# Layer 3's mask in the largest-score pass as a matmul with a plain maximum, and reciprocals of the weights' sums with queries in partitions

## The chip, the core and the metric

The kernel runs on one core of a Trainium2 chip. The metric is the device time of one execution in microseconds; for the kernel before there are three executions and one profiled one. TensorE is the matrix engine, VectorE, ScalarE and GpSimd work on 128 partitions each, and SyncE (SP) issues most DMAs. In the profile's rows they are PE (PEld for its weight loads), DVE, ACT, POOL and SP.

## What is computed

Four layers run over x of shape (8, 256, 128), with a context of shape (8, 512, 128). Each is a gated cross-attention and a gated feed-forward part, both on a layer-normalised x:

```python
x = x + tanh(g_xattn[l]) * attention_l(layernorm(x), ctx, ctx, ...)
x = x + tanh(g_ffn[l]) * feed_forward_l(layernorm(x), ...)
```

Layers 2 and 3 are what the change touches. Both have 16 heads of 8 features, 256 queries and 512 keys to a batch. Layer 2 has a mask of integers, a bias by position, and a softmax whose denominator has 1 added; layer 3 has two boolean masks:

```python
# layer 2
scores = where(mask == 0, -inf, q @ k.T / sqrt(8) + bias)
e = exp(scores - max(scores))
attn = e / (1.0 + sum(e))
# layer 3
energy = where(padding_mask & tri_mask, q @ k.T * 128**-0.5, finfo.min)
attn = softmax(energy)
```

Layer 2's feed-forward part is a mixture of 15 experts and a shared one, here all computed for all rows and weighed (16 passes for each group of 512 rows). Layer 3's is a linear layer with ternary weights and one common scale for its rounded input.

## The kernel before

Layer 0 and the setup run first, up to about 350 us. From then on `pipeline` (line 916) writes out one interleaved order of layers 1 to 3 in Python. The unit of work is (layer, batch, g), where g is one half of the heads: 48 units. Three streams go through the units: `prepare` (projections and loads of operands), four steps later `largest` (the row maxima of the scores), and four steps after that `attend` (scores again, now with keys in partitions, exponentials and the product with the values). A unit takes four steps of the loop at line 936, and in each step `largest` and `attend` come twice, each time with one score tile of 128x1024. Work that isn't of these streams is put in between: `later(1, f)` (line 979) puts a function on the list `due`, and `run_due` runs the list in the order in which it was filled, one step later, after the first `attend` tile of that step and ahead of its `largest` tile; `front` holds the preparation of the next batch, `back` the feed-forward parts (`int8`, `experts2`, `ternary`), one piece of each twice a step. VectorE, ScalarE, GpSimd and TensorE keep the order in which the instructions are written (`InOrder`, line 36, and `mm`, line 861).

PSUM has three score tiles (`sc`, 128x1024), one bank for small products (`pj`) and one for the product with the values (`av`). A score tile comes free when ScalarE's exponential or VectorE's maximum has read it; attend and largest tiles take turns.

`mask(layer, b)` (line 1397) makes the mask of a batch twice: `bq` with queries in partitions, two blocks of 512 keys, holding 0 or -2**100, and `bk`, its transpose, in bfloat16, with a second copy whose partition halves are swapped (two DMAs). `largest23` (line 1439) makes a score tile of 128 queries x 512 keys for two heads with two matmuls and then, for each head, calls `tensor_tensor_reduce` on VectorE: it adds `bq` to the scores and takes the maximum (each is followed by an instruction that reads the accumulator into `mx`). `largest_rows` (line 1168) turns `mx` by a transpose, splits it in two parts and writes them by DMA as rows of `qx`, so that the attend scores come with the maximum subtracted. `attend23` (line 1466) begins each of its score tiles with four 64x64 matmuls that add `bk` through blocks of an identity, then four score matmuls, and ScalarE's exponential.

`values_of_four` (line 1501) multiplies the exponentials by the values, 32 instructions in the trace for each call, twice a unit; the values are laid out with columns of ones beside them, so the sums of the weights stand in rows of the same result `oS`. After a batch's second unit `normalise` (line 1522) spreads these sums over the features' rows by the 0/1 matrix `sel` (result `pd`, features in partitions, 256 queries along the row), ScalarE copies them to `rec` (adding 1 in layer 2). One step later `scaled` takes the reciprocal of `rec` (128x256) on VectorE and GpSimd multiplies `oS` by it. One step after that `output23` projects. A float32 matmul stands as two instructions in the trace.

Of the kernel before, what the change touches and what calls it, by code (L numbers as in the profile page):

```python
# [10 lines left out]
BF16 = mybir.dt.bfloat16  # L11
# [8 lines left out]
P = 128  # L20
# [11 lines left out]
def bcast(ap, shape):  # L32
    return ap.to_broadcast(list(shape))
# [15 lines left out]
class Flamingo:  # L49
# [866 lines left out]
    def pipeline(self):  # L916
        nc, tc = self.nc, self.tc
        with ExitStack() as st:
            PS = bass.MemoryType.PSUM
            self.p_sc = st.enter_context(tc.tile_pool(name="p_sc", bufs=3, space=PS))  # L920
            self.p_pj = st.enter_context(tc.tile_pool(name="p_pj", bufs=1, space=PS))
            self.p_av = st.enter_context(tc.tile_pool(name="p_av", bufs=1, space=PS))
            self.po = st.enter_context(tc.tile_pool(name="pipe", bufs=2))
            units = [(layer, b, g) for layer in (1, 2, 3) for b in range(NB) for g in range(2)]
            self.due, self.soon, self.back, self.front, self.step, self.kept = [], [], [], [], 0, {}
            streams = {
                n: self.chain(f, units, wait)
                for n, f, wait in (("pr", self.prepare, 0), ("la", self.largest, 4), ("at", self.attend, 8))
            }
            self.fill_tile = lambda: self.t(self.po, "et", [P, 2, 2, S], bufs=5).rearrange(  # L930
                "p a b s -> p (a b s)"
            )[:, 0:SK]
            self.fill2(4)
            for _ in self.ahead(1, 0):
                pass
            for self.step in range(4 * len(units) + 12):

                next(streams["at"])
                self.run_due()
                next(streams["la"])  # L940
                self.run_soon()
                self.some(self.front)
                self.some(self.back)
                next(streams["at"])
                next(streams["pr"])
                next(streams["la"])
                self.fill2(1)
                self.some(self.front)
                self.some(self.back)
            while self.due or self.back:  # L950
                self.step += 1
                self.run_due()
                self.run_soon()
                self.some(self.back)
            self.ternary_end()
# [441 lines left out]
    def mask(self, layer, b):  # L1397


        nc, a = self.nc, self.a  # L1400
        bq = self.t(self.po, "bq", [P, 2, SK], BF16)
        bk = self.t(self.po, "m4", [P, 4, S], bufs=3).bitcast(BF16).rearrange("p (r k) n -> p r (k n)", r=2)

        def load(c):
            if layer == 2:
                tl = self.t(self.po, "mi", [P, SK], I32, bufs=1)
                nc.sync.dma_start(tl, a["mask"][b, c * P : (c + 1) * P, :])
                return tl
            if c == 0:
                tl = self.t(self.po, "pad", [P, SK], U8)  # L1410
                nc.sync.dma_start(tl, a["keep_bk"][b].partition_broadcast(P))
                return tl
            return got

        got = load(0)
        yield
        for c in range(2):
            if layer == 2:
                nc.vector.tensor_scalar(bq[:, c, :], got, 0.0, -BIG, ALU.is_equal, ALU.mult)
            else:  # L1420
                nc.vector.tensor_tensor(bq[:, c, :], self.triq[:, c, :], got, ALU.mult)
                nc.vector.tensor_scalar(bq[:, c, :], bq[:, c, :], 1.0, BIG, ALU.subtract, ALU.mult)
            if c == 0:
                got = load(1)
            yield
        pt = self.pj16()
        for k in range(4):
            for c in range(2):
                self.tp(
                    pt[:, k * S + c * P : k * S + (c + 1) * P], bq[:, c, k * P : (k + 1) * P], self.identb  # L1430
                )
        nc.scalar.copy(bk[:, 0, :], pt)
        for z in range(2):
            h, other = slice(64 * z, 64 * z + 64), slice(64 - 64 * z, 128 - 64 * z)
            nc.sync.dma_start(bk[h, 1, :], bk[other, 0, :])
        self.kept["mask", layer, b] = bq, bk
        yield

    def largest23(self, n, layer, b, g):
        nc = self.nc  # L1440
        qx, kx, _ = self.kept[n]
        bq, _ = self.kept["mask", layer, b]
        rows = 36 if layer == 2 else 32
        mx = self.t(self.po, "mx", [P, 2, 2, 2, 2])
        for j in range(4):
            for c in range(2):
                ps = self.sc()
                for z in range(2):
                    self.mm(
                        ps[:, z, :],  # L1450
                        self.packed(qx, z, 0, rows)[:, j, c * P : (c + 1) * P].bitcast(F32R),
                        self.packed(kx, z, 0, rows)[:, j, :].bitcast(F32R),
                    )
                for z in range(2):
                    junk = self.t(self.po, "junk", [P, SK], BF16, bufs=1)
                    nc.vector.tensor_tensor_reduce(
                        junk, ps[:, z, :], bq[:, c, :], 1.0, -3.0e38, ALU.add, ALU.max,
                        mx[:, c, j // 2, z, j % 2 : j % 2 + 1],
                    )
                if c and j % 2:  # L1460
                    self.later(1, self.largest_rows(
                        mx, j // 2, -1.0, lambda z, k: self.packed(qx, z, rows + k, 1)
                    ))
                yield

    def attend23(self, n, layer, b, g):
# [10 lines left out]
        for j in range(4):  # L1477
            for k2 in range(2):
                ps = self.sc()

                for z in range(2):
                    for o in range(2):
                        h = slice(64 * z, 64 * z + 64)
                        self.mm(
                            ps[64 * o : 64 * o + 64, z, :], self.identb[h, h],
                            bk[h, int(o != z), k2 * SK : (k2 + 1) * SK], True, False,
                        )
                for c in range(2):
                    for z in range(2):
                        at = (2 * k2 + c) * P  # L1490
                        self.mm(
                            ps[:, z, c * S : (c + 1) * S],
                            self.packed(kx, z, 0, rows)[:, j, at : at + P].bitcast(F32R),
                            self.packed(qx, z, 0, rows)[:, j, :].bitcast(F32R), False, c == 1,
                        )
                held[j, k2] = self.weights(ps, scale)
                if k2 and j % 2:
                    self.later(1, self.values_of_four(layer, b, g, j // 2, held, va, oS, oN))
                yield
# [21 lines left out]

    def normalise(self, layer, b, oS, oN):

        nc = self.nc
        pd = self.pj()
        for z in range(2):
            h = slice(64 * z, 64 * z + 64)
            for g in range(2):
                self.mm(pd[h, 0:S], self.sel[:, g, h], oS[:, g, :], g == 0, g == 1)
        rec = self.t(self.po, "rec", [P, S], bufs=1)  # L1530
        nc.scalar.activation(
            rec, pd[:, 0:S], AF.Identity, bias=self.ones[:, 0:1] if layer == 2 else 0.0
        )

        def scaled():
            nc.vector.reciprocal(rec, rec)
            nc.gpsimd.tensor_tensor(oN, oS, bcast(rec.unsqueeze(1), [P, 2, S]), ALU.mult)
            self.later(1, lambda: self.output23(layer, b, oN))

        self.later(1, scaled)  # L1540
# [23 lines left out]
    def experts2(self, tb):  # L1564
# [36 lines left out]
        def hidden(e):  # L1601
            ps = self.sc()
            self.mm2(ps[:, 0, :], self.f2_w[:, 0, e, :], xT)
            return ps
# [15 lines left out]
        def weighed(e, py):  # L1620
# [6 lines left out]
            for t in range(2, 4):  # L1627
# [2 lines left out]
                    self.x[:, t0 + t, :], ALU.mult, ALU.add,  # L1630
                )

        ps = hidden(0)
        pt = self.pj()
        for t in range(4):
            self.tp(pt[0 : E + 1, t * P : (t + 1) * P], comb[:, t, :], self.ident)
        hT = positive(0, ps)
        cT = self.t(po, "cT2", [E + 1, 512], bufs=1)
        nc.scalar.copy(cT, pt[0 : E + 1, :])
        yield  # L1640
        pb = self.sc()[:, 0, :]
# [10 lines left out]
        for e in range(E + 1):  # L1652
            ps = hidden(e + 1) if e < E else self.sc()
            output(e, hT, ps[:, 1, :])
            if e < E:
                hT = positive(e + 1, ps)
            weighed(e, ps[:, 1, :])
            yield


# [180 lines left out]
```

## Time and profile before

| What | Value |
|---|---|
| time, median of 3 runs | 1808.77 us (1801.66 to 1819.17) |
| time of the profiled execution | 1804.63 us |
| its span, first to last instruction | 1802.8 us |
| instructions in the trace | 33356 |
| mean granted TensorE clock | 0.905 |
| layers 1 to 3: first maxima with a mask (layer 2), layer 3's first and last | 922.2, 1358.7, 1757 us |
| attend's exponential, 128x1024 (ScalarE) | 1025 ns |
| reciprocal of 128x256 (VectorE), layers 2 and 3 | 16 of 1747 ns |

The span is that of the profiled execution, and the 1.8 us between it and that execution's time lie outside the instructions. In a group row of the profile come the line of the source (a helper's where it issues), engine, operation, out<-in by tile names, shapes and count; after the bar the busy time of the group, the mean duration of one in ns, and the idle time of the engine ahead of these. Matmuls that run side by side in parts of the array are counted once in the busy time. In a table of stretches each engine has its busy time and, in brackets, its instructions; PEclk is the share of the full clock that the throttle granted. A timeline row has the start, the duration, the engine, and in brackets the idle time ahead of it and what ended it.

### The profile page before, as it was taken

The page shows a single profiled execution, that of the slowest core. Times are in us where ns is not written, and L with a number is a line of the kernel's source. Part 1 is how long each engine was busy: PE and PEld are TensorE (multiplying, and loading weights), DVE is VectorE, ACT ScalarE, POOL GpSimd, SP SyncE. Part 2 cuts the span into 40 slices and gives each one's busy share as a digit, 9 for nine tenths or more (in the row PEclk, how much of TensorE's full clock was granted, in tenths as well). Part 3 has the DMA queues.
Part 4 walks back from the last instruction along what each step waited for, and adds up shares of the span by engine and source line. Part 5 has one row for each costly group of instructions (what it writes and reads, how often), then busy time and mean ns, then how long its engine had stood idle before and what let it go on. Part 6 is the DMA issues. An engine that isn't in the chain of part 4 may idle for free.

```text
span 1802.8 us, 33356 instructions
## 1 busy us (share of the span) xinstructions
PE 1570.0 (87%) x12368; PEld 787.8 (44%) x12368; DVE 1160.3 (64%) x2667; ACT 749.2 (42%) x1244; POOL 741.0 (41%) x1140
## 2 busy tenths in 40 slices
PE   5878578689999999999988889889898999899995
PEld 2333226134544545445554445445444455444442
DVE  7997642245677677676686666575665756666663
ACT  3443332343333232333333545555545555444443
POOL 4896221234656566565562231222232323322211
PEclk9896788899999999999998988989989899888876
DMA  5453232722221122122113331222121211222200
GB/s 190 150 166 113 94 127 76 237 99 100 75 73 54 48 78 77 48 55 94 51 40 104 85 91 44 68 69 54 50 54 37 65 46 44 63 63 63 66 17 25
DMA packets 67974, 142.04 MB, mean 79 GB/s; under 512 B 12882, under 2 KB 28515, under 8 KB 61156
## 3 DMA queue, kind: packets, MB, share of 16 engines
q1 hardware_dynamic: 65842, 136.22, 24.8%
q0 software_dynamic: 1536, 3.15, 1.3%
q8 instruction: 98, 1.61, 0.4%
q10 hardware_dynamic: 434, 0.54, 0.1%
q14 instruction: 64, 0.52, 0.1%
HBM read 83.50 MB, written 51.38 MB: 75 GB/s over the span
## 4 chain that ended last, share of the span: by engine, by line
PE 59%; DVE 20%; issue 6%; ACT 5%; POOL 5%; DMA 3%; SPq 1%; ACTq 0%; DVEq 0%; POOLq 0%
PE sc L863 31%; PE av L863 14%; PE pj L863 8%; DVE junk L46 4%; PE pj L867 3%; DVE ps L46 2%; DVE rec L46 2%; DVE pj L46 2%; DVE x L46 2%; DVE nm L46 1%; PE fl L863 1%; POOL k L46 1%; ACT et L46 1%; DMA kx<-k 1%; ACT total L46 1%
## 5 line engine op out<-in xcount | busy, mean ns | idle before, releaser
L46 ACT ACTIVATE et<-sc 128x1024 f32<-128x1024 f32 (+1 forms) x403 | 404.5, 1005 | 460.8 <-PE sc L863 434.5
L46 DVE CUSTOM_DVE_ANT_0 junk<-sc,bq 128x512 bf16<-128x512 f32 x512 | 350.9, 685 | 43.7 <-PE sc L863 30.0
L863 PE MATMUL av<-et,va 128*32 128x256 f32 (+1 forms) x3072 | 286.1, 439 | 0.8 <-DVE aT L46 0.8
L863 PE MATMUL sc<-qx,kx 64*128 64x256 f32 (+2 forms) x2048 | 275.8, 369 | 3.8 <-DMA qx<-ms 3.8
L863 PE MATMUL sc<-kx,qx 64*128 64x512 f32 (+2 forms) x1024 | 276.5, 576 | 0.4 <-ACT et L46 0.4
L46 POOL TENSOR_TENSOR k<-et 128x512 f32<-128x512 f32 x128 | 162.6, 1271 | 175.4 <-ACT et L46 174.4
L46 DVE TENSOR_REDUCE nm<-sc 128x2 f32<-128x1024 f32 x128 | 156.0, 1219 | 109.8 <-PE sc L863 109.8
L863 PEld LDWEIGHTS sc<-qx,kx 64*128 64x128 f32 (+2 forms) x2048 | 184.0, 197 | 92.5 <-issue 72.3
L863 PEld LDWEIGHTS av<-et,va 128*32 128x32 f32 (+1 forms) x3072 | 139.1, 133 | 113.2 <-issue 55.2
L46 POOL TENSOR_TENSOR x<-row,x 128x256 f32<-128x256 f32 x76 | 55.4, 729 | 274.8 <-ACT row L46 261.5
L46 DVE SCALAR_TENSOR_TENSOR ms<-pj,ms 4x256 fp32r<-4x256 f32 x96 | 39.5, 411 | 186.1 <-ACT ms L46 186.1
L863 PE MATMUL sc<-m,identb 64*64 64x512 bf16 x1024 | 115.0, 438 | 27.0 <-DVE mx L46 21.7
L863 PEld LDWEIGHTS sc<-kx,qx 64*128 64x128 f32 (+2 forms) x1024 | 90.3, 191 | 90.3 <-issue 69.4
L46 DVE RECIPROCAL rec<-av 128x256 f32<-128x256 f32 x64 | 111.8, 1747 | 0.0
L46 POOL TENSOR_TENSOR lnz<-lny 128x2 f32<-128x2 f32 (+1 forms) x129 | 25.0, 194 | 211.0 <-DVE lny L46 198.1
L46 DVE SCALAR_TENSOR_TENSOR x<-sc,comb,x 128x128 f32<-128x128 f32 x128 | 39.0, 346 | 100.1 <-ACT row L46 100.1
L863 PE MATMUL sc<-xT,wb 128*64 128x512 f32 x256 | 69.0, 614 | 24.3 <-DVE x L46 22.4
L46 ACT ACTIVATE total<-sc,f_b 128x512 f32<-128x512 f32 x64 | 44.0, 687 | 106.6 <-PE sc L863 106.6
L46 POOL TENSOR_TENSOR total<-k 128x512 f32<-128x512 f32 x64 | 81.4, 1271 | 5.0
L46 POOL TENSOR_TENSOR aT<-aT,rec 128x512 f32<-128x512 f32 x16 | 20.3, 1271 | 145.0 <-DVE rec L46 145.0
L863 PEld LDWEIGHTS <-identb 64*64 64x64 bf16 x1024 | 34.9, 107 | 95.3 <-issue 89.5
L863 PEld LDWEIGHTS sc<-wb,total 128*64 128x64 f32 x1024 | 61.7, 137 | 33.5 <-issue 33.5
(275 smaller groups left out, 2319.7 us busy)
## 6 DMA issues: line engine op xcount, KB each, us to landing
kx<-k SPq DMA_DIRECT2D x16, 1024.0 KB
va<-v SPq DMA_DIRECT2D x16, 1024.0 KB
k<-fill SPq DMA_DIRECT2D x46, 256.0 KB
v<-fill SPq DMA_DIRECT2D x45, 256.0 KB
pd<-k SPq DMA_DIRECT2D x16, 512.0 KB
kx<-pd SPq DMA_DIRECT2D x64, 128.0 KB
kx<-pd SPq DMA_DIRECT2D x128, 64.0 KB
qx<-pd SPq DMA_DIRECT2D x128, 64.0 KB
```

The lines of the kernel that those rows point to most:

```text
L46: return lambda *args, **kw: self.tc.keep_in_program_order(v(*args, **kw))
L863: self.nc.tensor.matmul(out, lhsT, rhs, start=start, stop=stop)
L867: self.tc.keep_in_program_order(self.nc.tensor.transpose(out, in_, ident))
```

## The change

- **Mask in largest-score tiles of layer 3.** The four mask matmuls of `attend23` become a method `masked`, and `largest23` calls it ahead of its two score matmuls for layer 3, except while the experts run (a flag `in_experts`, set from the first hidden product of `experts2` to its last but one step). In these tiles one `tensor_reduce` with max over 128x2x512 takes the place of the two `tensor_tensor_reduce`. The mask tile `bq` gets a second copy with swapped halves, by two more DMAs, in layer 3.
- **Reciprocals.** `normalise` now makes the sums with queries in partitions: `oS` is the stationary operand and every eighth column of `sel` (16 of them) the moving one. VectorE adds 1 or 0 and takes the reciprocal of 128x32. `scaled` widens each value to 8 columns on ScalarE (128x256), TensorE turns the two blocks against the identity, ScalarE copies the result, and GpSimd multiplies as before. This is for layers 2 and 3.
- **Room.** `pad` shares the tile of layer 2's integer mask, and `cT` that of `xn2`.

```diff
@@ mask
-        bq = self.t(self.po, "bq", [P, 2, SK], BF16)
+        bq = self.t(self.po, "bq", [P, 2, 2 * SK], BF16)
+        bqc = [bq[:, 0, c * SK : (c + 1) * SK] for c in range(2)]
...
-                tl = self.t(self.po, "pad", [P, SK], U8)
+                tl = self.t(self.po, "mi", [P, SK], I32, bufs=1)[:, 0 : SK // 4].bitcast(U8)
...
             h, other = slice(64 * z, 64 * z + 64), slice(64 - 64 * z, 128 - 64 * z)
+            if layer == 3:
+                nc.sync.dma_start(bq[h, 1, :], bq[other, 0, :])
             nc.sync.dma_start(bk[h, 1, :], bk[other, 0, :])
...
+    def masked(self, ps, b2, at):
+        for z in range(2):
+            for o in range(2):
+                h = slice(64 * z, 64 * z + 64)
+                self.mm(
+                    ps[64 * o : 64 * o + 64, z, :], self.identb[h, h], b2[h, int(o != z), at : at + SK],
+                    True, False,
+                )
@@ largest23
                 ps = self.sc()
+                by_pe = layer == 3 and not self.in_experts
+                if by_pe:
+                    self.masked(ps, bq, c * SK)
                 for z in range(2):
                     self.mm(
                         ps[:, z, :],
                         self.packed(qx, z, 0, rows)[:, j, c * P : (c + 1) * P].bitcast(F32R),
-                        self.packed(kx, z, 0, rows)[:, j, :].bitcast(F32R),
+                        self.packed(kx, z, 0, rows)[:, j, :].bitcast(F32R), not by_pe, True,
                     )
-                for z in range(2):
+                if by_pe:
+                    nc.vector.tensor_reduce(mx[:, c, j // 2, :, j % 2], ps, AX.X, ALU.max)
+                for z in () if by_pe else range(2):
@@ normalise
-        for z in range(2):
-            h = slice(64 * z, 64 * z + 64)
+        for c in range(2):
             for g in range(2):
-                self.mm(pd[h, 0:S], self.sel[:, g, h], oS[:, g, :], g == 0, g == 1)
-        rec = self.t(self.po, "rec", [P, S], bufs=1)
-        nc.scalar.activation(
-            rec, pd[:, 0:S], AF.Identity, bias=self.ones[:, 0:1] if layer == 2 else 0.0
+                self.mm(
+                    pd[:, 16 * c : 16 * c + 16], oS[:, g, c * P : (c + 1) * P], self.sel[:, g, 0:P:8],
+                    g == 0, g == 1,
+                )
+        rec = self.t(self.po, "rec16", [P, 2, 16])
+        nc.vector.tensor_scalar(
+            rec.rearrange("p c h -> p (c h)"), pd[:, 0:32], 1.0 if layer == 2 else 0.0, None, ALU.add
         )
+        nc.vector.reciprocal(rec, rec)
 
         def scaled():
-            nc.vector.reciprocal(rec, rec)
-            nc.gpsimd.tensor_tensor(oN, oS, bcast(rec.unsqueeze(1), [P, 2, S]), ALU.mult)
+            wide = self.t(self.po, "recw", [P, 2, P], bufs=1)
+            nc.scalar.copy(
+                wide.rearrange("p c (h f) -> p (c h) f", f=8),
+                bcast(rec.rearrange("p c h -> p (c h)").unsqueeze(2), [P, 32, 8]),
+            )
+            pr = self.pj()
+            for c in range(2):
+                self.mm2(pr[:, c * P : (c + 1) * P], wide[:, c, :], self.ident)
+            rows = self.t(self.po, "rec", [P, S], bufs=1)
+            nc.scalar.copy(rows, pr[:, 0:S])
+            nc.gpsimd.tensor_tensor(oN, oS, bcast(rows.unsqueeze(1), [P, 2, S]), ALU.mult)
             self.later(1, lambda: self.output23(layer, b, oN))
@@ experts2
+        self.in_experts = True
         ps = hidden(0)
...
-        cT = self.t(po, "cT2", [E + 1, 512], bufs=1)
+        cT = self.t(po, "xn2", [P, 4, D], bufs=1).rearrange("p t d -> p (t d)")[0 : E + 1, :]
...
             weighed(e, ps[:, 1, :])
+            self.in_experts = e < E
             yield
```

## The prediction

> **What bounds the kernel now.** I read the page first: busy shares and the chain that ended last.
>
> ```profile
> PE 1570.0 (87%) x12368; PEld 787.8 (44%) x12368; DVE 1160.3 (64%) x2667; ACT 749.2 (42%) x1244; POOL 741.0 (41%) x1140
> ...
> PE 59%; DVE 20%; issue 6%; ACT 5%; POOL 5%; DMA 3%; SPq 1%; ACTq 0%; DVEq 0%; POOLq 0%
> ```
>
> TensorE leads on both counts, but this is an average over stages, so I went to layer 3 alone. The scores of the largest-score pass run there from 1358.7 to 1757 us in 128 tiles, 8 to a unit of (batch, half of the heads). Without experts beside them, units alternate:
>
> ```profile
> core 0: us, PE busy (x) PEld busy (x) DVE busy (x) ACT busy (x) POOL busy (x), PEclk, DMA share, GB/s
> ...
> 1650.70:1670.70 20.00, 18.54 (x203) 10.00 (x202) 15.18 (x43) 11.72 (x19) 1.66 (x3) 1.00 0.25 69
> 1670.70:1695.00 24.30, 22.79 (x155) 9.75 (x154) 15.54 (x46) 10.07 (x14) 11.23 (x33) 0.65 0.23 60
> ```
>
> In both TensorE is busy 93% and VectorE 76% and 64%. The second has fewer matmuls yet takes longer: its granted clock is 0.65. What TensorE waits for between 1562 and 1758 us is little:
>
> ```profile
> engine line waited for: us in total, times, longest us
> PE sc L863 <- DVE mx L46: 9.1, 20, 0.6
> PE pj L867 <- DVE ms L46: 2.1, 4, 0.7
> ```
>
> So VectorE is near the bound only in short stretches of bare score tiles. One such stretch, with the reciprocal beside it, in the timeline:
>
> ```profile
> 1657.44 0.49 PE L863 MATMUL sc<-kx,qx 32*128 32x512 f32 x2
> ...
> 1658.13 0.08 DVE L46 DVE_READ_ACCUMULATOR2_ANT mx<- 128x1 f32 x1
> 1658.27 0.41 PE L863 MATMUL sc<-m,identb 64*64 64x512 bf16 x4 [0.33 <-DVE mx L46]
> ...
> 1658.61 0.50 PE L863 MATMUL sc<-qx,kx 34*128 34x256 f32 x4
> ...
> 1659.04 1.93 PE L863 MATMUL av<-et,va 128*32 128x256 f32 x32
> ...
> 1659.21 1.02 ACT L46 ACTIVATE et<-sc 128x1024 f32<-128x1024 f32 x1 [0.64 <-PE sc L863]
> ...
> 1659.71 1.75 DVE L46 RECIPROCAL rec<-rec 128x256 f32<-128x256 f32 x1
> ```
>
> One 0.33 us wait for the maximum, then the value products (av) follow, and the 1.75 us reciprocal lies wholly beside their 1.93 us and the rows behind them.
>
> **Part 1, the mask of the largest-score pass, on VectorE.** The rows that price it:
>
> ```profile
> L46 DVE CUSTOM_DVE_ANT_0 junk<-sc,bq 128x512 bf16<-128x512 f32 x512 | 350.9, 685 | 43.7 <-PE sc L863 30.0
> L46 DVE TENSOR_REDUCE nm<-sc 128x2 f32<-128x1024 f32 x128 | 156.0, 1219 | 109.8 <-PE sc L863 109.8
> L863 PE MATMUL sc<-m,identb 64*64 64x512 bf16 x1024 | 115.0, 438 | 27.0 <-DVE mx L46 21.7 <-ACT et L46 3.1 <-DVE x L46 2.0
> L46 DVE DVE_READ_ACCUMULATOR2_ANT mx<- 128x1 f32 x512 | 41.5, 81 | 0.0
> L863 PE MATMUL pj<-wr,xT 128*128 128x15 f32 x32 | 4.6, 278 | 0.0
> L863 PE MATMUL pj<-wp,ctxT 128*64 128x128 f32 x256 | 17.5, 279 | 0.0
> ```
>
> Per tile VectorE loses 2 x (685 + 81) = 1532 ns and gains one maximum over 128x1024, which is layer 1's row of 1219 ns: 0.31 us less. How many tiles? The flag leaves out those between an expert's start and its last but one step; counting the experts' matmuls between tiles gives 28 left out, 100 changed: 31 us less VectorE work. As VectorE isn't the bound, that is worth only the waits above: 9.1 us, and about 2 in the earlier changed tiles, **-11 us**.
>
> **Part 1 on TensorE.** Each changed tile gets four 64x64 mask matmuls of the very form of the third row. Taken from start to start, the group of four before the attention scores takes 0.34 us at full clock (1658.27 to 1658.61 above) and 0.57 at half (1587.69 to 1588.26 in the timeline). Of the 100 tiles 78 start at full clock, 22 at half: 78 x 0.34 + 22 x 0.57 = **+39 us**, in TensorE's own order, with nothing to hide behind in units that are 93% busy. Below it can't cost nothing, as the bare stretches leave only the 11 us already taken; above, if all ran at half clock, 57. With the waits gone: **+28 us**.
>
> **Part 2, the reciprocals (layers 2 and 3, 16 batches).** VectorE loses 1.75 us a batch and gains an addition and a reciprocal over 32 columns; no row is that small with 32, but the maximum's followers with 60 columns take 0.22 each, so 0.4 at most. TensorE: before, 8 instructions of 256 columns, 1.09 us busy in the timeline. After, 8 with a 128-column weight and 16 moving columns, nearest to the router's 128x15 (4.6 / 32 = 0.144 each, 1.15 us), and 8 that turn the widened rows (17.5 / 256 = 0.068 each, 0.55 us). That is +0.6 us a batch. ScalarE has two copies of 128x256 (0.37 each) for one of 0.38, with room.
>
> The order matters more. The reciprocal and the multiply were on VectorE and GpSimd, with no TensorE step between. Now `scaled` has ScalarE's widening copy, then TensorE's transposes, which wait for that copy, and TensorE keeps its order. `scaled` was put on the list before the values of the next half of the heads, so it runs ahead of av. ScalarE has, in the same order, the exponential of the tile just scored ahead of the copy. In the timeline av could start at 1659.04; the exponential ends at 1660.23; with 0.37 for the copy and two hand-overs of 0.04 the transposes start at 1660.68. **TensorE stands 1.6 us**, and behind it wait av, then the turning of the maxima, then the next scores. Beside experts the exponential ends 1.1 to 1.5 us after av's start, so 1.6 to 1.9. From below it is nothing if ScalarE had done the exponential by then, which the row excludes; from above 1.9. I take 1.6 for 15 batches: 15 x (1.6 + 0.6) = +33. VectorE catches up in that pause and has no long reciprocal, so I take 0.4 us a batch of later waits for it away, an estimate from the 0.33 wait above: -6. The last batch is alone at the end, where the chain goes through 0.38 + 1.75 us of ScalarE and VectorE: about 0.4 + 0.37 + 0.55 + 0.37 instead, -0.5. Sum **+26 us**.
>
> **Part 3, what costs nothing.** Two more DMAs a batch on SP's queue (the other halves of bq), just ahead of the mask's own copy, which takes 1.17 us for two; the mask is prepared about a unit ahead (20 us) and kx and qx of the next unit queue behind. If that cover fails, about 1.2 us a batch, 9 in all. The shared tile for pad is read 40 us before the next load needs it, and cT in place of xn2 was last read before it.
>
> **The clock.** Windows between changes of the granted clock are 3.4 us long. In a row:
>
> ```profile
> 1581.60:1585.10 3.50, 2.88 (x28) 1.42 (x24) 2.42 (x7) 1.68 (x3) 2.48 (x13) 0.99 0.01 2
> 1585.10:1588.50 3.40, 3.40 (x14) 0.92 (x14) 2.73 (x10) 1.71 (x2) 2.01 (x3) 0.50 0.45 121
> 1588.50:1591.90 3.40, 3.40 (x26) 1.62 (x30) 2.72 (x8) 1.75 (x2) 0.21 (x2) 0.50 0.72 176
> ```
>
> TensorE is busy all through the second and third, and stays at half. It is back at full only after the next window, with 28 of av's matmuls. The Trainium skill, page "TensorE: Matmul & The Clock Gate", Part 1, says that about 3.4 us of sustained work give the full clock and an idle window takes it away. By that rule more matmuls would lift the slow units: of the 110 us at half clock in the changed stretch 42% would be saved (0.34 for 0.57, 0.43 for 0.73, 1.87 for 3.57), 46 us. By the rows, windows that are full of masks and thin scores don't count as work; what returns the clock are full-row matmuls such as av. The measurement decides: I take no gain. The sum by the rule would be 23 + 26 - 46 = +3, by the rows +54.
>
> **Sum.** Span 1802.8 + 28 + 26 = 1856.8, with 1.8 around it (1804.63 less 1802.8) 1858.6. The median of the runs shown is 4 us above the profiled one, so I write **1860**.
>
> **The rivals.**
> 1. *Clock lost as well.* In the full-clock units the window at 1653 has no av; the selection matmuls, 256 columns each, carry it, and the change cuts them to 16. With the pause of 1.6 us it may fall to half until the next av: 6.8 us at half lose 2.9; in some 8 batches 23 us, 1882. For: the window before a fall has next to no av. Against: projections in it stay.
> 2. *The pause is hidden* by waits that would follow anyway: 28 + 15 x 0.6 - 6 = +31, 1836. Against: the slow waits in the table are short.
> 3. *Clock kept, on the other side.* The masks count as work and hold the full clock: +3, 1807, the same. It decides if nearly all 110 us at half turn full (about 54 / 0.42 = 129 would be needed to pay for the whole sum; 49 / 0.42 = 117 with the masks at 0.34). Faster by over 1% takes the pause hidden too (1807 - 24 = 1783).
> 4. *It doesn't do what it says:* if VectorE's maximum took over 1.53 us no VectorE time is saved. The layer 1 row of 1219 is the same form, so this is left at a few in a hundred, and its sum, 1870, lies in the range.
>
> **Chances.** 1860 with its own range 1845 to 1875: 0.52. Clock lost 0.22, pause hidden 0.14, clock kept 0.08, kept and pause hidden 0.04. A measurement of this kernel can tell about 1% from no change. Faster 0.05, same 0.09, slower 0.86. The range leaves out the two clock-kept cases and the ends: 1822 to 1895.
>
> **What would show it.** Maxima of about 1219 ns, 100 of them; the old ones down from 512 to 312; mask matmuls 1024 + 400; before the transposes a TensorE gap of some 1.6 us that ends with ScalarE's copy; units of 20.0 and 24.3 us at about 24 and 27; clock about 0.80 in 1562 on. Wrong if the slow units come out at clock near 1.0, or if no gap stands ahead of av.

## The result and the profile after

The changed kernel takes 1871.38 us (median of 4 runs, 1868.42 to 1877.61) against 1806.46 before (now the median of 4): a ratio of 1.0353, 95% interval 1.029 to 1.0415. It was forecast at 1860. The trace after is of the slowest of its four executions (1877.61), the trace before of one at 1804.63. The engines stand in the same order, with TensorE busy 87% of the span as before:

```profile
PE 1628.2 (87%) x12896; PEld 818.4 (44%) x12896; DVE 1130.6 (60%) x2383; ACT 754.6 (40%) x1260; POOL 743.2 (40%) x1140
...
PE 59%; DVE 18%; issue 7%; POOL 6%; ACT 6%; DMA 3%; SPq 0%; ACTq 0%; DVEq 0%; POOLq 0%
```

VectorE has 30 us less to do and the kernel is slower. To see where, I cut both traces at the first score matmul of each unit of the largest-score pass (16 units a layer, of 8 tiles) and compared unit by unit. Layer 1 agrees to 0.1 us in sum. Layer 2, of which only the reciprocals changed, is 39.6 us longer; layer 3 is 21.4 longer. Inside layer 3 the two kinds of unit went opposite ways: the first halves of the heads are 23.6 us shorter together, the second halves 45.0 longer. The stretch table of the changed kernel, one unit of each kind:

```profile
1654.50:1673.10 18.60, 18.25 (x190) 8.28 (x186) 15.85 (x21) 10.36 (x14) 11.03 (x31) 1.00 0.27 74
1673.10:1700.90 27.80, 25.44 (x244) 12.74 (x240) 13.14 (x22) 11.90 (x20) 2.11 (x6) 0.82 0.26 62
```

A unit of the kind that took 24.3 us at clock 0.65 before now takes 18.6 at 1.00, with more matmuls; one of the kind that took 20.0 at 1.00 now takes 27.8 at 0.82. I had forecast about 27 for the first and about 24 for the second.

The groups by shape show the operations as they were priced, and what TensorE waits for shows the pause:

```profile
L46 DVE TENSOR_REDUCE mx<-sc 128x2 f32<-128x1024 f32 x100 | 121.5, 1217 | 24.1 <-PE sc L863 23.9
L863 PE MATMUL sc<-bq,identb 64*64 64x512 bf16 x400 | 43.3, 423 | 0.0
L863 PE MATMUL pj<-sel,aT 128*128 128x16 f32 x128 | 18.4, 276 | 0.1
L863 PE MATMUL pj<-c_f,recw 128*64 128x128 f32 x128 | 14.5, 364 | 24.0 <-ACT recw L46 24.0
L46 ACT COPY recw<-rec 128x256 f32<-128x256 f32 x16 | 6.4, 402 | 1.5 <-DVE rec L46 1.5
```

A hundred maxima of 1217 ns, 400 mask matmuls, and 24.0 us in 16 batches, 1.5 each, in which TensorE stands for ScalarE's widening copy. One of these in the timeline:

```profile
1683.48 1.02 ACT L46 ACTIVATE et<-sc 128x1024 f32<-128x1024 f32 x1 [1.63 <-PE sc L863]
1684.40 0.40 ACT L46 COPY recw<-rec 128x256 f32<-128x256 f32 x1
1684.85 1.12 PE L863 MATMUL pj<-c_f,recw 128*64 128x128 f32 x8 [1.47 <-ACT recw L46]
...
1685.90 0.66 PE L863 MATMUL av<-et,va 128*32 128x256 f32 x4
```

The copy stands behind the exponential, the transposes behind the copy, and av behind the transposes, as the order of the code says.

The clock: in these windows of 3.4 us of the changed kernel av has no matmul, and yet the last is followed by a window at full clock.

```profile
1632.50:1635.90 3.40, 3.40 (x34) 2.08 (x30) 2.83 (x5) 1.19 (x2) 0.00 (x0) 1.00 0.62 171
1635.90:1639.30 3.40, 2.15 (x14) 0.92 (x10) 1.51 (x2) 2.01 (x3) 0.00 (x0) 0.50 0.56 134
1700.80:1704.20 3.40, 3.40 (x34) 1.58 (x30) 2.78 (x4) 1.64 (x4) 2.66 (x10) 1.00 0.01 2
1704.20:1707.60 3.40, 3.40 (x28) 1.28 (x28) 3.20 (x9) 2.41 (x3) 1.22 (x2) 1.00 0.58 138
```

With the mask identity's instructions alone, the first and the third of these stretches:

```profile
1632.50:1635.90 3.40, 1.33 (x16) 0.34 (x12) 0.00 (x0) 1.00 0.62 171
1700.80:1704.20 3.40, 1.86 (x20) 0.45 (x16) 0.00 (x0) 1.00 0.01 2
```

The first has 16 mask matmuls, and the clock falls after it; the third has 20, and it doesn't. Before, the window at 1581.6 had 8 (0.82 us), and it fell. Two windows prove little, so I counted all of layer 3 in the thirteen traces of this document. Every change of the clock lies on a grid of 3.41 us. Of the windows on this grid that run at full clock and in which no matmul of av starts, 71 of 180 are followed by half clock where 8 mask matmuls start in them, 11 of 102 where 12 start, 3 of 61 where 16 start, and none of 9 where 20 start. (The view also counts matmuls that cross an edge; by starts the two windows above have 12 and 16.)

### The profile page after: what moved, and what is told of

Its sections match the earlier page's. It is cut to its first block, busy times and chain, and to the rows that moved or that the text cites. A ratio compares the mean times of both kernels' runs of the same rounds, so it can differ in the third digit from the quotient of the medians.

```text
span 1875.8 us, 34105 instructions
## 1 busy us (share of the span) xinstructions
PE 1628.2 (87%) x12896; PEld 818.4 (44%) x12896; DVE 1130.6 (60%) x2383; ACT 754.6 (40%) x1260; POOL 743.2 (40%) x1140
## 3 DMA queue, kind: packets, MB, share of 16 engines
q1 hardware_dynamic: 67122, 138.32, 24.3%
## 4 chain that ended last, share of the span: by engine, by line
PE 59%; DVE 18%; issue 7%; POOL 6%; ACT 6%; DMA 3%; SPq 0%; ACTq 0%; DVEq 0%; POOLq 0%
PE sc L863 32%; PE av L863 13%; PE pj L863 8%; PE pj L867 3%; DVE ps L46 2%; DVE rec L46 2%; DVE pj L46 2%; ACT et L46 2%; POOL k L46 2%; DVE x L46 2%; DVE nm L46 2%; PE fl L863 1%; DVE junk L46 1%; ACT total L46 1%; ACT row L46 1%
## 5 line engine op out<-in xcount | busy, mean ns | idle before, releaser
L863 PE MATMUL av<-et,va 128*32 128x256 f32 (+1 forms) x3072 | 292.8, 450 | 0.8 <-DVE aT L46 0.8
L46 DVE CUSTOM_DVE_ANT_0 junk<-sc,bq 128x512 bf16<-128x512 f32 x312 | 213.5, 684 | 18.8 <-PE sc L863 12.1
L863 PEld LDWEIGHTS av<-et,va 128*32 128x32 f32 (+1 forms) x3072 | 141.5, 135 | 117.4 <-issue 62.4
L46 DVE TENSOR_REDUCE mx<-sc 128x2 f32<-128x1024 f32 x100 | 121.5, 1217 | 24.1 <-PE sc L863 23.9
L863 PE MATMUL sc<-xT,wb 128*64 128x512 f32 x256 | 72.6, 644 | 25.0 <-DVE x L46 21.7
L863 PEld LDWEIGHTS <-identb 64*64 64x64 bf16 x1424 | 43.4, 105 | 96.6 <-issue 85.6
L46 ACT ACTIVATE ms<-pj 4x256 fp32r<-4x256 f32 x96 | 35.7, 372 | 117.2 <-PE pj L867 107.4
```

The source lines that it names most:

```text
L46: return lambda *args, **kw: self.tc.keep_in_program_order(v(*args, **kw))
L863: self.nc.tensor.matmul(out, lhsT, rhs, start=start, stop=stop)
```

## The experiments

My theory before the runs was the prediction's, with masks that move no clock and a pause with its matmuls as the price of the reciprocals. The rival, read from the units above: masks hold the clock in the slow units and may gain by themselves; the pause and the missing selection columns lose the clock elsewhere. The table gives for each run the profile's difference to before in layers 2 and 3, from the first score matmul of layer 2's largest-score pass to the last of layer 3's (835.3 us before), and the timed ratio with its interval. The last column adds up, from the trace's record of the granted clock, the time that layer 2, layer 3's first halves and its second halves spent at half clock. Each row rests on one trace of the run and one of before. Masks alone (twice) and the masks with the old maximum leave layer 2's code as it was, and differ there by -5.7 to +0.6 us: smaller differences in layer 2 mean nothing.

| Kernel | layer 2 | layer 3, first halves | layer 3, second halves | sum, us | ratio | at half clock, us |
|---|---|---|---|---|---|---|
| before | | | | | | 78.5 / 95.6 / 14.7 |
| the change | +39.6 | -23.6 | +45.0 | +61.0 | 1.0353 (1.029 to 1.0415) | 136.5 / 16.6 / 61.9 |
| e1_masks | -1.6 | -23.5 | +3.5 | -21.6 | 0.9921 (0.9893 to 0.9949) | 81.9 / 17.1 / 0.0 |
| e1b_masks | -5.7 | -23.5 | +3.5 | -25.7 | 0.992 (0.9894 to 0.9946) | 68.3 / 17.1 / 0.0 |
| e2_recip | +35.5 | -9.2 | +35.3 | +61.6 | 1.0372 (1.0288 to 1.0455) | 122.9 / 61.4 / 64.9 |
| e5_pause | +26.0 | -0.3 | +25.9 | +51.6 | 1.032 (1.0248 to 1.0392) | 105.8 / 95.1 / 38.0 |
| e4_recip_after | +11.3 | -6.9 | +29.7 | +34.1 | 1.0154 (1.0079 to 1.023) | 85.3 / 74.5 / 67.6 |
| e4b_recip_after | +12.8 | -5.8 | +30.2 | +37.1 | 1.0194 (1.0142 to 1.0246) | 88.7 / 75.3 / 68.0 |
| e8_recip_columns | +25.4 | -9.2 | +13.5 | +29.7 | 1.0249 (1.0166 to 1.0333) | 109.2 / 62.4 / 9.3 |
| e8b_recip_columns | +17.2 | -2.3 | +14.6 | +29.5 | 1.0238 (1.0187 to 1.0288) | 92.2 / 88.0 / 11.0 |
| e3_both_after | +20.4 | -21.9 | +25.6 | +24.0 | 1.0143 (1.0066 to 1.0219) | 109.2 / 20.5 / 34.1 |
| e6_masks_old_max | +0.6 | -17.2 | +4.3 | -12.4 | 0.9966 (0.9937 to 0.9995) | 78.5 / 23.9 / 0.0 |
| e7_masks23 | +2.3 | -22.0 | +3.4 | -16.3 | 0.9912 (0.9887 to 0.9937) | 44.4 / 20.3 / 0.2 |

**Masks alone.** The change with `normalise` as it was before.

```diff
@@ normalise
-        for c in range(2):
+        for z in range(2):
+            h = slice(64 * z, 64 * z + 64)
             for g in range(2):
...
+                self.mm(pd[h, 0:S], self.sel[:, g, h], oS[:, g, :], g == 0, g == 1)
...
+            nc.vector.reciprocal(rec, rec)
+            nc.gpsimd.tensor_tensor(oN, oS, bcast(rec.unsqueeze(1), [P, 2, S]), ALU.mult)
```

> Part 1 alone: masks of the largest-score pass by TensorE with the plain maximum, reciprocals as before the change. The prediction's theory (masks cost TensorE 0.34 or 0.57 us a tile and move no clock): +28 us on 1806, about 1834. The rival read from the changed kernel's trace (a second set of masks holds the full clock in the units that were at 0.65, and costs about 2 us in the units at full clock): layer 3 gets shorter by 5 to 25 us, 1781 to 1801, and the slow units come out near 18.6 us at clock 1.00, the others near 22.

Measured: 1796.62 us, and a ratio of 0.9921 to the runs of before that were taken beside it on the same chip: a small gain, but its interval leaves out 1. The rival is right. Two units in the stretch table:

```profile
1595.90:1614.50 18.60, 18.25 (x190) 8.29 (x186) 15.79 (x21) 10.36 (x14) 11.05 (x31) 1.00 0.29 74
1614.50:1636.00 21.50, 20.95 (x236) 10.65 (x232) 14.18 (x21) 11.60 (x19) 2.04 (x5) 1.00 0.33 80
```

The full-clock unit pays about 1.5 us for 8 masks of 0.34 (2.7) less the waits for the maximum that are gone; the slow one turned full and gained 5.8.

> Masks alone once more, beside the others. If the gain is real: 0.985 to 0.995 of before, with layer 3's units 8, 10 and 12 at clock 1.00 and 18.6 us again.

Again 0.992, and again 20.0 us less in layer 3. The gain is real, and it is small because it lies in six of layer 3's units (2, 8, 10, 12, 14 and 15) and the others pay. A shift of the clock's grid against the program does not explain it: units 8, 10 and 12 have a clock of 0.65 to 0.84 in all seven traces without masks in layer 3 and of 0.92 to 1.00 in all six with them. By the times the gain is 0.8%, about 14 us, and by the traces 22 and 26; with one trace of before, the difference stays open.

**Masks on TensorE, VectorE as before.** Of the gain, what is the clock's and what is VectorE's?

```diff
+        self.zeros = self.t(one, "zeros", [P, SK], BF16)
+        nc.gpsimd.memset(self.zeros, 0.0)
...
-                if by_pe:
-                    nc.vector.tensor_reduce(mx[:, c, j // 2, :, j % 2], ps, AX.X, ALU.max)
-                for z in () if by_pe else range(2):
+                for z in range(2):
...
-                        junk, ps[:, z, :], bq[:, 0, c * SK : (c + 1) * SK], 1.0, ...
+                        junk, ps[:, z, :], self.zeros if by_pe else bq[:, 0, ...], 1.0, ...
```

> Masks by TensorE in layer 3 as in part 1, but VectorE keeps its old operation in these tiles (add and maximum for each head, with zeros in place of the mask), reciprocals as before: the masks on TensorE without any VectorE saving. If the gain of the masks alone (-22 us in layers 2 and 3) is the clock's, the slow units still come out at clock 1.00 and the gain is -10 to -20; what it lacks to -22 is VectorE's part. If the gain is VectorE's, it is gone: 0 to +20 with units at 0.65 or so again.

Measured: -12.4 in the profile, ratio 0.9966 (its interval just leaves out 1), slow units at 19.6 to 20.4 us and clock 0.92 to 1.00:

```profile
1632.00:1651.60 19.60, 18.66 (x188) 8.36 (x186) 16.84 (x45) 10.60 (x14) 11.39 (x34) 1.00 0.27 71
```

So work added to TensorE, with nothing taken from VectorE, shortened these layers. In layer 3 alone it is -12.9 against -20.0 with the plain maximum: the clock is the larger part, and about 7 us are VectorE's (19.6 against 18.6 us in a unit). TensorE's waits of its score tiles for the maximum fell as much without the plain maximum (21.7 us before to 9.6) as with it (9.8): beside the masks VectorE no longer holds TensorE up there, whichever operation it has.

**Masks in layer 2 too.**

```diff
-                by_pe = layer == 3 and not self.in_experts
+                by_pe = not self.in_experts
...
-            if layer == 3:
-                nc.sync.dma_start(bq[h, 1, :], bq[other, 0, :])
+            nc.sync.dma_start(bq[h, 1, :], bq[other, 0, :])
```

> Part 1 in layers 2 and 3 (masks by TensorE and the plain maximum outside the experts, with the second copy of the mask in both), reciprocals as before. If the masks hold the clock, layer 2's slow units (2, 4, 6, 10, 14 at 0.62 to 0.84) come out near 1.00 as well, layer 2 gets 10 to 20 us shorter, and the kernel stands at 0.98 to 0.987 of before. If layer 3's gain has to do with its own data, layer 2 gains nothing or loses 0.34 us a tile, up to 15 us.

A miss in time: layer 2 gained nothing (+2.3). Units 4 and 10 were 2.3 and 2.0 us shorter at a higher clock (1.00 and 0.92), but units 2 and 14 were 2.9 and 1.6 longer at 0.73 and 0.75, and four full-clock units (3, 5, 9 and 13) paid 6.0. The clock did move: half clock in layer 2 went from 78.5 us to 44.4, under the 68.3 to 81.9 of the runs that leave it alone. But 87 tiles got masks there, 30 us at 0.34, and that took back what the clock gave. The ratio, 0.9912, can't be told from the masks alone.

**Reciprocals alone.** The kernel before, with the changed `normalise`.

> Part 2 alone: reciprocals with queries in partitions, masks on VectorE as before. The prediction's theory (pause of 1.5 us and 0.6 us of matmuls a batch, less 0.4): +26, about 1832. The rival (the pause and the missing selection columns also lose the clock in the unit that holds them, as layer 2 of the changed kernel shows with +40 us in eight batches): +60 to +85, 1866 to 1891, with those units at 25 to 28 us and a clock of 0.7 to 0.8.

Measured: +61.6, ratio 1.0372. The whole loss of the change is here. TensorE stands 24.0 us for the copy, as in the change; the units of the selection go from 19.9 us at 1.00 to 25.7 at 0.80:

```profile
1642.00:1663.80 21.80, 18.68 (x155) 8.64 (x154) 15.44 (x46) 10.21 (x14) 11.75 (x33) 0.84 0.26 67
1663.80:1689.60 25.80, 22.81 (x211) 12.26 (x210) 13.84 (x44) 11.99 (x20) 1.66 (x3) 0.80 0.22 53
```

**The pause alone.** Selection and reciprocal as before, with a copy on ScalarE and transposes of it put where the change has them, their result unused.

```diff
         def scaled():
+            wide = self.t(self.po, "recw", [P, 2, P], bufs=1)
+            nc.scalar.copy(wide, oS[:, 0, :].rearrange("p (c d) -> p c d", c=2))
+            pr = self.pj()
+            for c in range(2):
+                self.mm2(pr[:, c * P : (c + 1) * P], wide[:, c, :], self.ident)
+            rows = self.t(self.po, "rows0", [P, S], bufs=1)
+            nc.scalar.copy(rows, pr[:, 0:S])
             nc.vector.reciprocal(rec, rec)
```

> The kernel before with the pause alone: ScalarE copies 128x256 of the unnormalised result and TensorE turns that copy at the place where the changed kernel turns the reciprocals; the turned copy is read by ScalarE and not used. Selection columns and VectorE's reciprocal stay. Pause and matmuls without loss of clock: 16 x (1.5 + 0.55), +33, 1839. If the pause alone loses the clock: +60 to +85. If the clock falls only with the selection columns gone: close to +33 with the units at clock 1.00.

Between the two: +51.6, of which about 33 are the pause (23.7 in its trace) and the transposes. A full-clock unit of layer 3 takes 23.4 us at clock 0.93, 3.4 over before: 2.05 by the pause and the transposes, the remaining 1.4 by the clock.

```profile
1661.90:1685.30 23.40, 20.46 (x211) 10.95 (x210) 15.19 (x43) 12.35 (x21) 1.66 (x3) 0.93 0.24 59
```

In both layers together 50 us more are at half clock, which at the forecast's 42% is an estimated 21 us.

**Reciprocals without the pause.** The turning is moved behind the next largest-score tile; TensorE's wait for the copy goes from 24.0 to 1.1 us. The cut is against the reciprocals alone.

```diff
+            def turned():
-            pr = self.pj()
+                pr = self.pj()
                 ...
+            self.soon.append(turned)
```

> Part 2 alone, with the turning of the widened rows put behind the value products and the next largest-score tile in TensorE's order, so that ScalarE's copy is long done: no pause, but the selection still has 16 columns in place of 256. If the pause is the cause of all, it is back at 1806 plus 16 x 0.6 less what VectorE gains, 1800 to 1816. If the missing columns lose the clock by themselves, 1830 to 1860, with the units of the selection still at a clock under 0.9.

Measured: +34.1, ratio 1.0154. So the pause and what hangs on it cost 27.5 us of the 61.6, and 34 stay though the pause is gone: the selection's units in layer 3 are at 0.61 to 0.86. Not all of the 34 is the clock. TensorE has about 10 us of matmuls more, and its small products wait longer for VectorE's `ms`, the split of the maxima (15.2 us against 9.5 before).

**The same with the columns added back.** Four selection matmuls of 256 columns write a part of the bank that nobody reads.

```diff
+        for z in range(2):
+            h = slice(64 * z, 64 * z + 64)
+            for g in range(2):
+                self.mm(pd[h, S : 2 * S], self.sel[:, g, h], oS[:, g, :], g == 0, g == 1)
```

> Part 2 without the pause, as in the run with the turning put behind, and with the old selection matmuls of 256 columns added back into a part of the bank that nobody reads. If the missing columns lost the clock there, the selection's units come back to 1.00 and stand about 1.7 us over before (1.1 for the added matmuls, 0.6 for the rest) in place of 4.0: layers 2 and 3 at +20 to +28 in place of +34, although TensorE has more to do. If the clock fell for another reason, it gets longer by the matmuls: about +34 + 16 = +50.

> Part 2 without the pause once more, timed beside the same with the selection's columns added back. Before: +34 us in layers 2 and 3 of one profile, ratio 1.0154. If the missing columns cost more clock than the added matmuls cost time, this one is the slower of the two by 3 to 10 us.

> Part 2 without the pause and with the columns added back, on the same chip as the run without them. The clock theory: the selection's units in layer 3 at 0.95 to 1.00 and about 2.2 us over before in place of 4 to 5; in all 3 to 10 us less than without the columns. If the phase of the clock's windows alone made the difference in the profile, it is slower by the matmuls, 10 to 17 us.

In both pairs the profile is shorter with more matmuls, by 4.4 and 7.6 us, although 16 x 1.1 = 17.6 us of them were added. But both profiles without the columns are of the slowest execution of their run (1852.95 against a median of 1844.41, 1856.02 against 1845.94), so the sums flatter the columns; the units and the clock tell more. The same unit in the second pair, first without, then with the columns:

```profile
1651.80:1675.80 24.00, 21.94 (x209) 11.82 (x208) 13.84 (x44) 11.95 (x20) 1.67 (x3) 0.86 0.24 57
```

```profile
1650.40:1672.50 22.10, 20.13 (x217) 11.37 (x216) 13.92 (x44) 11.79 (x20) 1.65 (x3) 1.00 0.26 63
```

So in layer 3 the missing columns cost the clock: in the second halves 67.6 and 68.0 us are at half without them, 9.3 and 11.0 with them. The windows say the same in both layers. Take the 3.41 us windows at full clock in which all 8 instructions of a selection start. With 256 columns, in six traces, half clock follows none of 68. With 16 columns it follows 39 of 50, and 24 of 34 in the three traces without a pause. With the columns added back it follows 3 of the 22 that hold all 8 added ones. As a whole it doesn't pay: in layer 2 it was 14 and 4 us longer and had more time at half clock, which stays open; and timed on one chip the columns took 1853.05 us against 1845.94, ratios 1.0238 and 1.0194 with intervals that overlap. My forecast that the kernel without them would be the slower by 3 to 10 us is not confirmed.

**The whole change without the pause.**

> The whole change, with the turning of the widened rows put behind the value products and the next largest-score tile. If the parts add up: masks alone -22 us in layers 2 and 3, part 2 without the pause +34, so +12 in these layers, a ratio near 1.007. If masks also hold the clock where the selection's columns are missing: the units at full clock of layer 3 lose at most 2 us each, the sum is -5 to +5. If the pause is what cost most in layer 3 whatever the masks do, layer 3 comes out near the masks alone (-20) and layer 2 near +11.

Measured: +24.0, ratio 1.0143 (1.0066 to 1.0219); the sum of the parts would be +12. Second halves are 5.2 us longer at 0.86 (units 7 and 11): masks don't hold the clock there. The best versions are the masks alone and the masks in both layers, which the times can't tell apart.

## Why the prediction was right in sum

- **The number by luck.** 1871.38 lies near 1860, but the account behind 1860 is wrong in its largest term. I had named a sign of that: slow units at a clock near 1.0. They came out at 1.00 and 18.6 us, and the clock from 1562 to 1758 us at 0.89, where I had written 0.80.
- **VectorE isn't the bound.** Right. But its saving was priced too high: 31 us for the masks and about 22 for the reciprocals. Masks alone took 9.3 us off VectorE (1160.3 to 1151.0), reciprocals alone 23.4 (to 1136.9); that both together come to 30 is chance. The sum 685 + 81 ns adds a read of the accumulator that overlaps its operation: the one that starts at 1657.51 in the trace before lasts 0.69, and its read starts at 1658.13. A tile's two operations with their reads take 1.43 us (1658.36 to 1659.79), not 1.53. Writing `bq` also took 6 us more (5.8 to 12.0). And the 11 us of waits were not what this saving is worth: they went without it too. By the masks with and without the old operation, the plain maximum is worth about 7 us.
- **Masks: 100 tiles, 0.34 us at full clock, 0.57 at half.** Right in the parts (340 and 570 ns, start to start, in the changed kernel too). Wrong as a sum: +28 was forecast, -21.6 and -25.7 measured alone. The step that failed is "windows that are full of masks and thin scores don't count as work". I had read it from windows with 8 mask matmuls at the most. With twice as many, few windows lose the clock. There the rule that I had set aside was the better guide, though not as it stands: a window with TensorE busy for all of its 3.4 us and 16 mask matmuls still lost the clock. Rival 3's mechanism was true of layer 3's first halves; it had no more than a chance of 0.08 since I took it for all the half-clock time or none.
- **The pause: 1.6 us a batch.** Right: 1.5 (24.0 / 16), by the mechanism named. The selection at 1.15 us was right (18.4 / 16); the transposes took 0.9 (14.5 / 16) in place of 0.55, some of them at half clock. The 6 us of waits for VectorE that I took away are not there: with reciprocals alone the waits of the score tiles for the maximum went from 21.7 to 20.3.
- **Reciprocals +26.** The step that failed is the clock, put at nothing: +61.6. Rival 1's mechanism, put at 23 us in 8 batches, acted in both layers. In the changed kernel layer 2 has 136.5 us at half clock against 78.5: 58 more, of which the forecast's 42% are 24 us lost. With 8 x (1.5 + 0.6) = 17 for pause and matmuls that makes 41, against 39.6 measured.
- **The sum.** The forecast's +54 had the clock at nothing: two errors of 50 and 36 us, masks forecast too dear and reciprocals too cheap, cancelled in part. They don't cancel to 61.0 by themselves, since the parts measured alone add up to 36 to 40. What is between lies mainly in layer 3. Its first halves had 9.2 us back with the reciprocals alone, and masks can't give the same half-clock time back twice; its second halves came out at 45.0 where 35.3 and 3.5 were measured alone. An estimate by terms: in layer 3 half clock went from 110 to 78.5 us, 13 us gained. Masks 100 x 0.34 - 11 = 23; reciprocals 24.0 + 16 x 0.6 - 1 = 33; clock 24 - 13 = 11. That is 67, and 61.0 was measured.
- **DMAs and shared tiles at nothing.** No wait of TensorE in the changed part of layer 3 names the mask's DMAs.

What stays open: the exact measure of a window's work. Of 180 windows with 8 masks and no av, 109 kept the clock, so what else is in a window counts too. The experiments show which way masks and selection columns move the clock, not by what weights.

## What to carry to other kernels

Price a TensorE edit twice, once by its instructions and once by what it does to the clock's windows on both sides: here 0.34 us of added masks a tile made units 5.8 us shorter, and a pause of 1.5 us a batch with 0.55 of transposes cost 3.2 a batch. Before an elementwise step is moved to TensorE, look at what stands ahead of its operand in the feeding engine's order, and put the matmul behind other work rather than ahead of it. Two changes measured together hid that one gains 0.8% and the other loses 3.7%: undo one part before either is judged.

## What the runs showed that I had not expected

- Removing columns can cost time with no one waiting: 240 columns fewer in each of 4 selection matmuls a batch, and units went from 19.9 to 24.0 us or, in some, to 30.6 at clock 0.61. With the columns back they took 22.1.
- Layer 0, the same in all these kernels, ended between 347 and 366 us in the profiles (351.2 before, 364.5 in the change). This is most of why the spans of the two profiles differ by 73.0 us and the layers that changed by 61.0.
